# Later blocks of the routed experts loaded by plain transfers, and a planner that ranks small products behind indirect transfers

## The chip, the cores and the metric

The kernel runs on one core of one Trainium2 chip, as one program. The metric is the device time of one execution in microseconds. The time before is the median of 13 executions.

## The reference

A decoder of four layers works on 2048 tokens (32 sequences of 64) of width 256, in float32. Each layer adds three parts to the residual, each on its layer-normed input: a mixer, a cross attention, and a feed-forward part.

```python
x = x + L0_attn(ln(x)); x = x + L0_xattn(ln(x), ctx); x = x + L0_ffn(ln(x))   # attention, 32 heads
x = x + L1_attn(ln(x)); x = x + L1_xattn(ln(x), ctx); x = x + L1_ffn(ln(x))   # state space mixer; 8 experts, top 2
x = x + L2_attn(ln(x)); x = x + L2_xattn(ln(x), ctx); x = x + L2_ffn(ln(x))   # state space mixer
x = x + L3_attn(ln(x)); x = x + L3_xattn(ln(x), ctx); x = x + L3_ffn(ln(x))   # attention; 64 experts, top 6, room for 128
```

The part that the change touches is the feed-forward of layer 1. A router picks for each token the two best of eight experts and weighs them by a softmax over those two. Each expert is a gated unit of inner width 256 (gate clamped from above at 7, up part clamped to -7 to 7, the product `(up + 1) * gate * sigmoid(1.702 * gate)`), and the token receives the weighted sum of its two experts' outputs.

## The kernel before

**Tiles and groups.** The 2048 tokens are 16 tiles of 128 rows. They go through the layers in three groups of 8, 6 and 2 tiles (`GROUPS`). While one group goes through the later part of the network (the experts of layer 1, layers 2 and 3), the next one goes through layers 0 and 1: `weave` records the two streams alternately. The last group computes all eight experts for all its tokens (`unit_L1_expert`); the first two groups use queues, and only those two are touched by the change.

**The queues of layer 1.** `plan_L1_ffn` makes five kinds of steps for a group of nt tiles:

- `unit_L1_route`, one for two tiles: the router, the two best experts, each token's place in its expert's queue, and two indirect transfers for each tile by GpSimd that scatter the normed rows into the DRAM tensor `queue`. An expert's queue has `cap` = 128 nt rows and was filled with zeros beforehand.
- `unit_L1_blocks`, once: a block is 128 rows of one expert's queue. There are `blocks_of(tiles)` blocks, 23 for 8 tiles and 19 for 6. Block b below 8 is the first block of expert b. Which expert the blocks from 8 on belong to depends on the tokens; this step computes it on VectorE from the experts' counts: for each later block its expert `ex`, the first row `at` of its part of the queue, and from these two tables of indices, `st["weights"]` and `st["rows"]`, with one index for each of the 128 partitions.
- `unit_L1_block`, one for each block: loads the expert's weights `w` (128 partitions of 1540 floats: gate and up, down, biases) from `f1_rows` and 128 rows `xs` from the queue, transposes the rows, computes the expert and stores its output to the DRAM tensor `result`. Blocks 0 to 7 load by plain transfers issued on SyncE (SP). The later blocks, 15 in the first group and 11 in the second, load by two indirect transfers issued on GpSimd (POOL), `nc.gather`, with the indices of the tables.
- `unit_L1_result`, one for each tile: gathers the two results of each token by two indirect transfers and adds them, weighted, to the residual.

Layer 3's experts use indirect transfers as well: 84 scatters into `slots` (6 a tile in the first two groups) and 64 scatters into `parts`. In all there are 256 indirect transfers, all issued on GpSimd, of which 52 are the later blocks' loads.

**Buffers.** Every tile of SBUF and PSUM is one of a few kinds with a fixed number of slots (`SLOTS`): 9 of kind w (the blocks' weights among them), 16 of kind b2 (the blocks' rows), 8 banks of PSUM (mm).

**The planner.** The code only records operations. `in_turns` then orders them: `Order.run` is a list scheduler with a cost for each operation (`duration`), which at each step takes the operation with the smallest key over all five engines; the key is the time at which it could start, with additions for changes of tile shape on TensorE (`SWITCH`) or of activation tables on ScalarE. An operation may go to TensorE, VectorE, ScalarE, GpSimd or SyncE, some to either of two. Where the plan leaves TensorE idle for more than 1.6 us, `fill` puts in a spare product (`spare_mm`) whose output nobody reads. The planner runs five times forwards with backward passes in between and keeps the shortest plan; `issue` writes the instructions in that order, each engine's in its own queue, which is worked through in order. Semaphores do the rest: where the plan's times are wrong, only the order stays.

**Names in the profile.** All instructions are written by one line of `issue`, so every row says L2500, and rows are told apart by the buffers' names: `L_block_w` and `L_block_b` are the block's weights and its other buffers, `L_blocks_sm` and `L_blocks_b` the tables of `unit_L1_blocks`, `queue`, `result`, `slots` and `parts` the DRAM tensors. The layer's number is left out of names, so `L_attn_mm` are products of several layers' attention; those of form 32*64 are the scores of layer 0, 128 products for one tile, each on one of four 32-row strips of the array. A float32 product has two records of weight load and two of matmul, a transpose one of each.

Of the kernel before, what the change touches and what calls it, by code (L numbers as in the profile page):

```python
# [23 lines left out]
ALU = mybir.AluOpType  # L24
AX = mybir.AxisListType

P = 128
# [422 lines left out]
        return lambda *args, **kw: self.rec.add([(self.name, method)], args, kw)  # L450


DMA = ("dma_start", "indirect_dma_start")
TABLES = {"Exp": 1, "Ln": 2, "Sigmoid": 3, "Silu": 4, "Sin": 4}


def part(method, args):

    if method == "transpose":
        return 128, 128  # L460
    return tuple(32 if n <= 32 else 64 if n <= 64 else 128 for n in (args[1].n, args[1].size()))


def duration(engine, method, args, kw):

    out = kw["out"] if "out" in kw else args[0]
    if method in DMA:
        return 0.45 if engine == "sync" else 1.28
    views = [v for v in [*args, *kw.values()] if isinstance(v, View)]
    n = max(v.size() for v in views)  # L470
    if engine == "tensor":
        k, m = part(method, args)
        if method == "transpose":
            return 0.109
        n = args[2].size()
        if m == 128:
            return max(0.223, n * 0.00167 + 0.004) if k > 32 else max(0.056, n * 0.00053)
        if k == 128:
            return max(0.058, n * 0.00083 + 0.003) if m == 64 else max(0.055, n * 0.00043 + 0.008)
        return n * 0.00042 + 0.002 if k == 64 else n * 0.00021 + 0.001  # L480
    small = any(v.size() == 1 and v.n > 1 for v in views) and n > 1
    psum = any(v.t.psum for v in views)
    full = sum(all(s for s, _ in v.dims) and v.size() == n for v in views[1:])
    if engine == "vector":
        if not psum and method in ("tensor_scalar", "tensor_copy", "tensor_scalar_add", "tensor_single_scalar"):
            return 0.16 + n * 0.00052 + 0.11 * small
        if method.startswith("reduce") and views[1].dims[-1][0] > 1:
            return 0.15 + n * 0.0017
        return 0.15 + n * 0.00104 + 0.06 * small
    if engine == "scalar":  # L490
        if method == "activation":
            return (0.17 if psum else 0.205) + n * 0.00083 + 0.18 * (small and psum)
        return 0.16 + n * 0.00084 + 0.1 * small
    if method == "memset":
        return 0.2 + n * 0.00066
    if ALU.pow in args:
        return 0.4 + 0.157 * n
    if method == "tensor_copy":
        return 0.25 + n * 0.001
    return 0.14 + n * (0.00174 if full < 2 else 0.0022)  # L500
# [17 lines left out]
NEAR = 10  # L518


def combines(op, engine, method):

    if engine == "gpsimd":
        return method == "tensor_tensor" and ALU.pow not in op.args
    return engine == "vector" and not any(v.t.psum for v in op.outs + op.ins if isinstance(v, View))


class Order:
    ENGINES = ("tensor", "vector", "scalar", "gpsimd", "sync")

    def __init__(self, ops, slots, horizon, spare):
        self.ops, self.slots, self.horizon, self.spare = ops, slots, horizon, spare
        self.free_at = {e: 0.0 for e in self.ENGINES}
        self.table, self.moved = 0, 0.0
        self.part = None

        self.until = {"vector": 0.0, "gpsimd": 0.0}

        self.free = {tag: [(0.0, k) for k in range(n)] for tag, n in slots.items()}

        events = {tag: [] for tag in slots}
        for o in ops:
            for t in o.tiles:
                if t.tag in slots and t.first == o.at:
                    events[t.tag].append((o.at, 0, t))
                if t.tag in slots and t.last == o.at:
                    events[t.tag].append((o.at, 1, t))
        self.events = {tag: sorted(ev, key=lambda e: e[:2]) for tag, ev in events.items()}

        work, self.pos = 0.0, []  # L550
        for o in ops:
            self.pos.append(work)
            if o.ways[0][0] == "tensor":
                work += duration("tensor", o.ways[0][1], o.args, o.kw)
# [31 lines left out]
    def fill(self, o, start):  # L586
# [9 lines left out]
        t.slot = free.pop(at[-1])[1]  # L596
        return op

    def elsewhere(self, o, engine, since, end):


        for w, m in o.ways:
            if w != engine:
                other = max(self.free_at[w], since) + duration(w, m, o.args, o.kw)
                gain = {"vector": 1.0, "gpsimd": -1.0}[w] if {w, engine} == {"vector", "gpsimd"} else 0.0
                if other + gain < end:
                    return True
        return False

    def run(self):  # L610
# [10 lines left out]
        while not all(done[oldest:]):  # L621
            limit = self.pos[oldest] + self.horizon
            best = None
            for e in self.ENGINES:
                now, seen, first = self.free_at[e], 0, 1e9
                for o in ready[e]:
# [13 lines left out]
                    if e == "tensor":  # L640
                        if start == now:
                            first = min(first, self.pos[o.at])
                        if part(method, o.args) != self.part:
                            key += SWITCH
                            cost += SWITCH
                        elif self.pos[o.at] > first + NEAR:
                            key += SWITCH
                        elif self.part != (128, 128):
                            key = start
                    if e == "scalar":  # L650
                        table = TABLES.get(getattr(o.args[2], "name", "") if method == "activation" else "", 0)
                        if table and table != self.table:
                            key += 1.3
                            cost += 1.3
# [36 lines left out]
            if e == "scalar":  # L691
                m = next(m for w, m in o.ways if w == e)
                table = TABLES.get(getattr(o.args[2], "name", "") if m == "activation" else "", 0)
                self.table = table or self.table
            if e == "tensor":
                self.part = part(o.ways[0][1], o.args)
            lat = latency(e, o)
            if o.ways[0][1] in DMA:
                v = next(v for v in o.outs + o.ins if isinstance(v, View) and v.dtype != I32)
# [87 lines left out]
class Net:  # L787
# [985 lines left out]
    def unit_L1_blocks(self, st):  # L1773
# [15 lines left out]
        nc.vector.tensor_tensor(tmp, low, tb(nb, 8), ALU.mult)  # L1789
        nc.vector.reduce_sum(end, tmp, AX.X)  # L1790

        ex, before, last, at = self.sm(n), self.sm(n), self.sm(n), self.sm(n)
        over = self.tmp(n, 8)
        nc.vector.tensor_tensor(over, bc(io, 2, 8), tb(end, n), ALU.is_ge)
        nc.vector.reduce_sum(ex, over[:, :, :7], AX.X)
        st["weights"] = self.sm(n, dtype=I32)
        nc.vector.tensor_scalar(st["weights"], ex, float(P), self.k("row"), ALU.mult, ALU.add)
        nc.vector.tensor_tensor(over[:, :, :7], over[:, :, :7], tb(nb[:, :7], n), ALU.mult)
        nc.vector.reduce_sum(before, over[:, :, :7], AX.X)
        nc.vector.tensor_tensor(over, bc(ex, 2, 8), tb(e8, n), ALU.is_equal)  # L1800
        nc.vector.tensor_tensor(over, over, tb(count, n), ALU.mult)
        nc.vector.reduce_sum(last, over, AX.X)

        nc.vector.scalar_tensor_tensor(at, io, 1.0, before, ALU.add, ALU.subtract)
        nc.vector.tensor_scalar(at, at, float(P), self.k("row"), ALU.mult, ALU.add)
        nc.vector.scalar_tensor_tensor(at, last, -1.0, at, ALU.add, ALU.min)
        nc.vector.tensor_single_scalar(at, at, 0.0, ALU.max)
        st["rows"] = self.sm(n, dtype=I32)
        nc.vector.scalar_tensor_tensor(st["rows"], ex, float(st["cap"]), at, ALU.mult, ALU.add)
# [15 lines left out]
    def unit_L1_block(self, b, st):  # L1825
        nc = self.nc
        w, xs = self.w(1540), self.b2(256)
        if b < 8:
            self.load(w, self.ins["f1_rows"][b * P : (b + 1) * P, :])
            self.load(xs, st["queue"](b * st["cap"], b * st["cap"] + P))  # L1830
        else:
            nc.gather(w, self.ins["f1_rows"], st["weights"][:, b - 8 : b - 7])
            nc.gather(xs, st["queue"](), st["rows"][:, b - 8 : b - 7])
        gu, dn, bias = w[:, :1024].rearrange("p (c n) -> p c n", c=2), split(w[:, 1024:1536], 2), w[:, 1536:]
        xT = self.b2(2, P)
        ps = split(self.mm()[:, :256], 2)
# [643 lines left out]
def issue(tc, order, slots):  # L2480
# [3 lines left out]
    with ExitStack() as ctx:  # L2484
# [9 lines left out]
        for op, e in order:  # L2494
            for t in op.tiles:
                if t.real is None:
                    tag = t.tag if t.slot is None else f"{t.tag}_{t.slot}"
                    t.real = pools[t.pool].tile(t.shape, t.dtype, name=t.name, tag=tag)
            method = next(m for w, m in op.ways if w == e)
            done = getattr(getattr(nc, e), method)(*map(real, op.args), **{k: real(v) for k, v in op.kw.items()})  # L2500
            if op.group is not None:
                op.name = done.ins.name
                tc.add_to_no_dep_group(op.group, done.ins)
                tc.declare_no_dep(done.ins, group=op.group, reason="rows of their own")

            for o in op.behind:
                if o.group != op.group and (e, o.name) not in waited:
                    waited.add((e, o.name))
                    tc.add_manual_dep(done.ins, o.name, sync, reason="rows")
# [99 lines left out]
```

## Time and profile before

| | |
|---|---|
| median of 13 executions | 2955.72 us (2953.68 to 2965.59) |
| profiled execution | 2956.93 us |
| its span, first to last instruction | 2955.2 us |
| mean granted TensorE clock | 0.979 |
| busy PE / PEld | 2885.5 us (98%) / 2401.2 us (81%) |
| busy DVE / ACT / POOL | 2046.7 us (69%) / 1415.4 us (48%) / 1485.1 us (50%) |
| DMA | 257.26 MB, mean 87 GB/s |
| queue q1, plain transfers (hardware_dynamic) | 204.73 MB, 19.9% of 16 engines |
| queue q0, indirect transfers (software_dynamic) | 48.01 MB, 4.7% |
| queue q8, instructions | 230 packets, 3.77 MB, 0.5% |
| spare products | 138 records, 34.3 us of PE |

PE is TensorE's matmul, PEld its weight load, DVE VectorE, ACT ScalarE, POOL GpSimd, SP SyncE. A group's line has the engine, the operation, the buffers written and read, the number of instructions, and their times. In a timeline, the bracket at the end of a line is the engine's idle time before the instruction and what ended it; "issue" stands for idle time in which the engine waited for nothing that the profile shows. The granted clock is the share of TensorE's full clock; in this trace it is either 1 or 0.5 at a time, and a mean over a stretch lies between.

### The profile page before, as it was taken

The numbers are of one execution on the slowest core, as the hardware profiler recorded it, in microseconds if no ns is written. First come the engines' busy times: TensorE is split into PE (matmuls) and PEld (weight loads), VectorE is DVE, ScalarE is ACT, GpSimd is POOL, SyncE is SP. The second block draws the span as 40 slices with busy tenths as digits, with TensorE's granted clock in tenths as the row PEclk, the third lists the DMA queues.
The fourth block names the chain that finished last, engine by engine and source line by source line (L and its number), as shares of the span: only waits on it lengthen the run. The fifth ranks groups of instructions, "written<-read, shape, count | busy, mean of one in ns | idle before, by whom it ended". The sixth has DMA issues, their size and how long they took to land.

```text
span 2955.2 us, 70820 instructions
## 1 busy us (share of the span) xinstructions
PE 2885.5 (98%) x29064; PEld 2401.2 (81%) x29064; DVE 2046.7 (69%) x5046; ACT 1415.4 (48%) x2665; POOL 1485.1 (50%) x1334
## 2 busy tenths in 40 slices
PE   9999999999999999999999999999999999998899
PEld 8888888787878888878888788878897878887677
DVE  5554337775666557765588998887756778898863
ACT  2224225565543233454466666665335565466460
POOL 5542143222765545523667536676554557555561
PEclk8999999999999999999999999999999999999899
DMA  5002421301251244412001010022374122221255
GB/s 187 13 10 94 169 72 43 144 1 45 104 210 44 62 139 137 138 38 81 32 30 38 25 42 30 6 89 85 114 261 142 56 95 81 63 76 39 78 162 204
DMA packets 112966, 257.26 MB, mean 87 GB/s; under 512 B 26309, under 2 KB 73688, under 8 KB 100228
## 3 DMA queue, kind: packets, MB, share of 16 engines
q1 hardware_dynamic: 97860, 204.73, 19.9%
q0 software_dynamic: 14784, 48.01, 4.7%
q8 instruction: 230, 3.77, 0.5%
q14 instruction: 92, 0.75, 0.1%
HBM read 177.34 MB, written 78.77 MB: 87 GB/s over the span
## 4 chain that ended last, share of the span: by engine, by line
PE 86%; DVE 8%; issue 2%; ACT 2%; POOL 1%; DMA 1%; POOLq 0%; DVEq 0%; ACTq 0%
PE L_xattn_mm L2500 13%; PE ssm_heads_mm L2500 10%; PE cross_out_mm L2500 9%; PE L_attn_mm L2500 9%; PE pair_mm L2500 9%; PE L_ffn_mm L2500 5%; PE rope_mm L2500 5%; PE turn_mm L2500 4%; PE L_block_mm L2500 3%; PE cross_scores_mm L2500 2%; PE L_dense_mm L2500 2%; DVE ssm_heads_b L2500 2%; PE heads_mm L2500 1%; PE L_experts_mm L2500 1%; PE small_scores_mm L2500 1%
## 5 line engine op out<-in xcount | busy, mean ns | idle before, releaser
L2500 PE MATMUL pair_mm<-norm_b,load_ssm_w 128*128 128x256 f32 x1280 | 306.3, 381 | 1.5 <-DVE L_attn_b L2500 0.8
L2500 PEld LDWEIGHTS pair_mm<-norm_b,load_ssm_w 128*128 128x128 f32 x1280 | 236.0, 190 | 41.8 <-issue 10.5
L2500 ACT COPY turn_b<-turn_mm 128x512 f32<-128x512 f32 x264 | 145.2, 592 | 149.8 <-PE turn_mm L2500 148.1
L2500 DVE SCALAR_TENSOR_TENSOR ssm_heads_b<-pair_mm,load_ssm_wp,ssm_heads_b 128x252 f32<-128x252 f32 (+2 forms) x480 | 196.1, 463 | 21.5 <-ACT ssm_heads_b L2500 19.8
L2500 POOL TENSOR_TENSOR L_xattn_sm<-L_xattn_sm,__init___consts 128x8 f32<-128x8 f32 (+2 forms) x64 | 190.1, 2975 | 29.5 <-DVE L_xattn_sm L2500 26.8
L2500 ACT ACT_TABLE_LOAD x147 | 188.6, 1283 | 24.3 <-PE ssm_heads_mm L2500 7.0
L2500 ACT COPY L_xattn_b<-L_xattn_mm 128x512 f32<-128x512 f32 x172 | 101.2, 591 | 164.6 <-PE L_xattn_mm L2500 153.6
L2500 POOL TENSOR_TENSOR norm_sm<-norm_sm,__init___consts 128x1 f32<-128x1 f32 (+1 forms) x149 | 94.1, 637 | 153.9 <-DVE norm_sm L2500 124.5
L2500 PE MATMUL ssm_heads_mm<-load_ssm_w,ssm_heads_b 128*128 128x256 f32 x640 | 164.7, 387 | 1.2 <-POOL L_xattn_b L2500 1.2
L2500 PE MATMUL rope_mm<-norm_b,load_L_attn_w 128*128 128x128 f32 x1280 | 163.8, 281 | 0.7 <-ACT L_block_b L2500 0.5
L2500 PEld LDWEIGHTS rope_mm<-norm_b,load_L_attn_w 128*128 128x128 f32 x1280 | 155.9, 196 | 7.6 <-issue 4.6
L2500 POOL TENSOR_TENSOR ssm_heads_b<-ssm_heads_b,ssm_heads_b 128x1024 f32<-128x1024 f32 x31 | 75.4, 2437 | 146.2 <-DVE ssm_heads_b L2500 102.1
L2500 PEld LDWEIGHTS ssm_heads_mm<-load_ssm_w,ssm_heads_b 128*128 128x128 f32 x640 | 115.0, 190 | 31.8 <-issue 17.8
L2500 POOL TENSOR_TENSOR L_attn_b<-rope_b 128x256 f32<-128x256 f32 x147 | 105.4, 741 | 60.0 <-DVE rope_b L2500 51.0
L2500 ACT COPY norm_b<-norm_mm 128x256 f32<-128x256 f32 (+1 forms) x128 | 54.3, 437 | 168.0 <-PE norm_mm L2500 120.6
L2500 POOL TENSOR_TENSOR heads_b<-heads_b,heads_sm 128x1024 f32<-128x1024 f32 x49 | 96.3, 1973 | 75.9 <-DVE heads_sm L2500 54.5
L2500 PEld LDWEIGHTS L_xattn_mm<-norm_b,load_L_xattn_w 128*128 128x128 f32 x1024 | 121.9, 192 | 7.7 <-issue 5.0
L2500 PE MATMUL L_xattn_mm<-norm_b,load_L_xattn_w 128*128 128x128 f32 x1024 | 127.2, 276 | 0.8 <-ACT heads_b L2500 0.8
L2500 PE MATMUL L_xattn_mm<-norm_b,units_L_xattn_w 128*128 128x128 f32 x1024 | 124.8, 279 | 0.0
L2500 PEld LDWEIGHTS L_xattn_mm<-norm_b,units_L_xattn_w 128*128 128x128 f32 x1024 | 121.9, 195 | 3.0 <-issue 1.5
L2500 PE MATMUL cross_out_mm<-load_L_xattn_w,cross_out_b 128*128 128x256 f32 x512 | 122.3, 384 | 0.1
L2500 ACT ACTIVATE ssm_heads_b<-ssm_heads_b 128x512 f32<-128x512 f32 (+1 forms) x120 | 91.8, 773 | 62.6 <-DVE ssm_heads_b L2500 41.9
(432 smaller groups left out, 7783.7 us busy)
## 6 DMA issues: line engine op xcount, KB each, us to landing
queue<-far_w SPq DMA_DIRECT2D x14, 1024.0 KB, 12.6
L_block_w<-in_f_rows SPq DMA_DIRECT2D x16, 770.0 KB, 4.6
load_ssm_w<-in_s_in SPq DMA_DIRECT2D x12, 1024.0 KB, 7.2
parts<-far_w SPq DMA_DIRECT2D x10, 1024.0 KB, 13.8
slots<-far_w SPq DMA_DIRECT2D x16, 548.0 KB, 6.7
L_experts_b<-slots SPq DMA_DIRECT2D x32, 274.0 KB, 3.7
units_L_xattn_w<-kept_x SPq DMA_DIRECT2D x8, 1024.0 KB, 7.8
L_parts_b<-parts SPq DMA_DIRECT2D x14, 512.0 KB, 6.1
```

Source lines behind the costliest of these rows:

```text
L2500: done = getattr(getattr(nc, e), method)(*map(real, op.args), **{k: real(v) for k, v in op.kw.items()})
```

## The change

It has two parts. In the first, the later blocks' weights and rows are loaded by `dma_from`, a plain transfer on SyncE whose first row is read at run time: SyncE reads one index from the table into a register, and the transfer's source begins at that row. The tables now hold each block's first row (the per-partition addition goes), the clamp to the last token of the expert is replaced by a clamp to the last 128 rows of the expert's part of the queue, and the four instructions that computed and applied `last` go. A transfer may thus read queue rows that no token was written to; they hold zeros, and no token takes its result from them. The planner counts 0.9 us on SyncE for such a transfer.

In the second, the planner keeps a list `rows` of the planned indirect transfers and a model of TensorE's instruction supply: 80 instructions in stock, refilled at 11.3 a microsecond during such a transfer. A product is called small if its instructions (4, or 2 for a transpose) are more than that rate delivers in its planned duration. While the latest planned indirect transfer runs, a small product's key rises by `AVOID` = 3.0 us plus the modelled wait; an indirect transfer's key rises by `HOLD` = 1.5 us if TensorE's latest product was small.

```diff
-DMA = ("dma_start", "indirect_dma_start")
+DMA = ("dma_start", "indirect_dma_start", "dma_from")
...
-        return 0.45 if engine == "sync" else 1.28
+        return 0.9 if method == "dma_from" else 0.45 if engine == "sync" else 1.28
...
+AHEAD, SLOW = 80, 11.3
+AVOID, HOLD = 3.0, 1.5
+def instructions(method):
+    return 2 if method == "transpose" else 4
...
+    def supply(self, start):
+        ahead, at = self.ahead, self.at
+        for a, b in self.rows:
+            if b > at and a < start:
+                if a > at:
+                    ahead, at = AHEAD, a
+                b = min(b, start)
+                ahead, at = min(AHEAD, ahead + (b - at) * SLOW), b
+        if at < start:
+            ahead = AHEAD
+        return ahead
...
+                        if self.rows and self.rows[-1][1] > start:
+                            n = instructions(method)
+                            wait = max(0.0, n - self.supply(start)) / SLOW
+                            if n > duration(e, method, o.args, o.kw) * SLOW:
+                                key += wait + AVOID
+                            start += wait
+                    if e == "gpsimd" and method in DMA and self.light:
+                        key += HOLD
...
+            if e == "gpsimd" and m in DMA:
+                self.rows = [r for r in self.rows if r[1] > self.free_at["tensor"] - 5.0] + [(start, got)]
             if e == "tensor":
-                self.part = part(o.ways[0][1], o.args)
+                self.part, n = part(o.ways[0][1], o.args), instructions(m)
+                self.light = n > duration(e, m, o.args, o.kw) * SLOW
+                self.ahead, self.at = max(0.0, self.supply(start) - n), start
...
-        nc.vector.tensor_scalar(st["weights"], ex, float(P), self.k("row"), ALU.mult, ALU.add)
+        nc.vector.tensor_single_scalar(st["weights"], ex, float(P), ALU.mult)
...
-        nc.vector.tensor_tensor(over, bc(ex, 2, 8), tb(e8, n), ALU.is_equal)
-        nc.vector.tensor_tensor(over, over, tb(count, n), ALU.mult)
-        nc.vector.reduce_sum(last, over, AX.X)
...
-        nc.vector.tensor_scalar(at, at, float(P), self.k("row"), ALU.mult, ALU.add)
-        nc.vector.scalar_tensor_tensor(at, last, -1.0, at, ALU.add, ALU.min)
+        nc.vector.tensor_scalar(at, at, float(P), float(st["cap"] - P), ALU.mult, ALU.min)
...
-            nc.gather(w, self.ins["f1_rows"], st["weights"][:, b - 8 : b - 7])
-            nc.gather(xs, st["queue"](), st["rows"][:, b - 8 : b - 7])
+            at = slice(b - 8, b - 7)
+            nc.sync.dma_from(out=w, in_=self.ins["f1_rows"], row=st["weights"][:1, at], last=7 * P)
+            nc.sync.dma_from(out=xs, in_=st["queue"](), row=st["rows"][:1, at], last=8 * st["cap"] - P)
...
+            if method == "dma_from":
+                at = nc.sync.value_load(kw.pop("row"), min_val=0, max_val=kw.pop("last"))
+                kw["in_"], method = kw["in_"][bass.ds(at, P), :], "dma_start"
```

More of the change, by code (lines that the diff above doesn't have):

```diff
@@ L534, in __init__ @@
         self.table, self.moved = 0, 0.0
-        self.part = None
+        self.part, self.light = None, False
         self.until = {"vector": 0.0, "gpsimd": 0.0}
+        self.rows, self.ahead, self.at = [], AHEAD, 0.0
         self.free = {tag: [(0.0, k) for k in range(n)] for tag, n in slots.items()}
@@ L1790, in unit_L1_blocks @@
         nc.vector.reduce_sum(end, tmp, AX.X)
-        ex, before, last, at = self.sm(n), self.sm(n), self.sm(n), self.sm(n)
+        ex, before, at = self.sm(n), self.sm(n), self.sm(n)
         over = self.tmp(n, 8)
@@ L2499, in issue @@
             method = next(m for w, m in op.ways if w == e)
-            done = getattr(getattr(nc, e), method)(*map(real, op.args), **{k: real(v) for k, v in op.kw.items()})
+            kw = {k: real(v) for k, v in op.kw.items()}
+            if method == "dma_from":
+                at = nc.sync.value_load(kw.pop("row"), min_val=0, max_val=kw.pop("last"))
+                kw["in_"], method = kw["in_"][bass.ds(at, P), :], "dma_start"
+            done = getattr(getattr(nc, e), method)(*map(real, op.args), **kw)
             if op.group is not None:
```

## The prediction

> **What bounds the kernel now.** I read the page first, then the table of stages, then the views of the gathers, PE's waits and the timeline. All times are of one execution: 2956.93 us, span 2955.2 us, so 1.7 us lie around the span. The median of the runs before is 2955.72 us, 1.2 us lower; I carry differences from the trace over to that median. A difference below 0.2% (5.9 us) counts as no change, about what measurement can tell here.
>
> The page (busy time, granted clock in 40 slices, chain that ended last):
>
> ```profile
> PE 2885.5 (98%) x29064; PEld 2401.2 (81%) x29064; DVE 2046.7 (69%) x5046; ACT 1415.4 (48%) x2665; POOL 1485.1 (50%) x1334
> ...
> PEclk8999999999999999999999999999999999999899
> ...
> PE 86%; DVE 8%; issue 2%; ACT 2%; POOL 1%; DMA 1%; POOLq 0%; DVEq 0%; ACTq 0%
> ```
>
> TensorE is the bound; GpSimd, SyncE and transfers hardly lie on the chain. So work taken off GpSimd is worth nothing by itself: gains come from PE's idle 70 us (2955.2 - 2885.5) and from lost clock. The table of stages (us; busy per engine; granted clock; DMA share, GB/s) shows where:
>
> ```profile
> 930.00:1250.00 320.00, 309.67 (x3540) 274.66 (x3539) 214.11 (x524) 105.45 (x200) 166.43 (x167) 0.93 0.33 109
> ...
> 1925.00:2270.00 345.00, 339.08 (x3274) 284.39 (x3273) 233.03 (x645) 159.49 (x319) 211.63 (x194) 0.98 0.43 148
> ...
> 2680.00:2955.20 275.20, 248.93 (x2366) 196.54 (x2348) 183.69 (x599) 118.82 (x243) 130.93 (x134) 0.93 0.37 125
> ```
>
> These are the three stages with indirect transfers. Lost clock there: 0.07 x 320 = 22 us, 0.02 x 345 = 7 us, 0.07 x 275 = 19 us. The last has also 26 us of idle PE. This is the ground the change can win or lose on.
>
> **Part 1: 52 gathers become plain transfers.** The tile view of the gathers and the list of DMA issues (last number: us to landing):
>
> ```profile
> L2500 POOL DMA_INDIRECT L_block_w<-in_f_rows,L_blocks_sm x26: 940/961/1947, 1084.0 to 2190.5; - x26
> ...
> L2500 POOL DMA_INDIRECT L_block_b<-queue,L_blocks_sm x26: 945/971/1162, 1015.2 to 2193.9; - x26
> ...
> L_block_w<-in_f_rows SPq DMA_DIRECT2D x16, 770.0 KB, 4.6
> ...
> L_block_w<-in_f_rows,L_blocks_sm POOLq DMA_INDIRECT x26, 7.3
> ```
>
> Removed from GpSimd: 26 x 0.96 + 26 x 0.97 = 50 us, in two stretches (about 1015 to 1182 and 2153 to 2195). GpSimd's waits put 19.0 us before weight gathers for a buffer that PE frees; products queued behind them on GpSimd (halves of rope, row scalings) come free earlier. On the path this is 0: POOL is 1% of the chain. What counts is where PE stood still. PE's waits in 1000:1200, and two lines of the timeline:
>
> ```profile
> PE L_attn_mm L2500 <- issue: 2.2, 1, 2.2
> PE L_block_mm L2500 <- DVE L_block_b L2500: 2.0, 1, 2.0
> PE L_block_mm L2500 <- DMA L_block_w<-in_f_rows,L_blocks_sm: 1.3, 1, 1.3
> ```
>
> ```profile
> 1113.43 3.16 DVE L2500 SCALAR_TENSOR_TENSOR L_block_b<-L_block_b,L_block_b 128x256 f32<-128x256 f32 x2
> ...
> 1116.40 1.97 PE L2500 MATMUL L_block_mm<-L_block_w,L_block_b 128*128 128x256 f32 x8 [2.04 <-DVE L_block_b L2500]
> ```
>
> (a) 1.3 us waiting for gathered weights. A plain load lands 7.3 - 4.6 = 2.7 us sooner, so the wait goes: 1.3 us, between 0 and 1.3. (b) A VectorE product took 2.8 us instead of its median 0.42 beside the gather at 1113.05, and PE waited 2.0 us for it: 2.0 us, between 0 and 2.0, since GpSimd's own products can stretch it as well. (c) The 2.2 us of "issue" at 1101.4 to 1103.6 are a late fetch of PE's instructions. The DMA queues from 1092.7 to 1101.1, and behind it from 1101.1 to 1105.5:
>
> ```profile
> q0 software_dynamic: 329, 1.68, 57.6%
> q1 hardware_dynamic: 720, 0.87, 29.4%
> ```
>
> ```profile
> q8 instruction: 2, 0.03, 3.0%
> ```
>
> While gathers hold q0, no instruction fetch starts for 8.4 us; then two come, and PE has run dry. A 10.2 us stretch (1101.0 to 1111.2) at clock 0.50 follows, 5.1 us lost. But small products run dry without gathers too: the same strip group at 161.3 waited 1.60 us for instructions and lost no clock. So of 2.2 + 5.1 = 7.3 us I give the gathers 2.2 - 1.6 + 5.1 = 5.7, between 0 and 7.3. In the second stretch PE waits for no transfer: 0. Sum: 1.3 + 2.0 + 5.7 = 9.0 us, between 0 and 10.6.
>
> Added: 52 register reads and 52 transfers on SyncE. The trace of before shows no register read. Bounds: one issue on SyncE (0.33 us, the plain weight load) and the landing of a small transfer (2.7 us, the block's rows from the queue); I take 1.5, 52 x 1.5 = 78 us of SyncE over some 210 us, where it mostly waits (ACT's L_block_b alone holds it 77 us in 1000:1200). Behind the new waits on SyncE stand result stores, context loads and the next mixer's weights; PE waits for those late by no line of this stretch. So 0 on the path; if that cover fails, a late load costs about the 1.3 us of (a), and four of them 5 us. (The Trainium skill, "DMA: Bandwidth & Descriptors", section "Latency and other measured facts", puts a register load's floor near 600 ns; by that SyncE would get an estimated 31 us instead. No run here shows it.) The eight small VectorE instructions dropped in the two block plans, 0.16 to 0.28 us each, are off the path: 0.
>
> **Part 2: the planner's ranking.** While a planned indirect transfer runs, products that it calls small (128 columns, strips, transposes) get 3 us on their key and a modelled stall; a GpSimd transfer gets 1.5 us after such a product. No instruction is added; the written order changes. The model says 11.3 instructions per us, with 80 in stock. The timeline beside the last experts' scatters speaks against that rate:
>
> ```profile
> 2859.24 3.67 PEld L2500 LDWEIGHTS L_experts_mm<-L_experts_b,load_L_experts_w 128*32 128x32 f32 x136 [0.33 <-ACT L_experts_b L2500]
> ```
>
> ```profile
> 2858.82 0.97 POOL L2500 DMA_INDIRECT parts<-L_experts_b,L_experts_sm  x1 [0.30 <-DMA parts<-L_experts_b,L_experts_sm]
> 2860.10 0.97 POOL L2500 DMA_INDIRECT parts<-L_experts_b,L_experts_sm  x1 [0.30 <-DMA parts<-L_experts_b,L_experts_sm]
> ```
>
> 136 weight loads with their matmuls are 272 instructions in 3.67 us, 74 per us. So the cost avoided is rare, tied to large gathers, and Part 1 takes those away. (The Trainium skill, "Runtime: NRT & Kernel Launch", section "Instruction fetch mechanics", says a sequential program's fetch is hidden; by it the ranking would win 0. The trace agrees beside these scatters but not at 161.3 and 1101.) The one place left where it may help: strips beside the result gathers at 1205 wait 1.2 us and are followed by 6.9 us at clock 0.51, together 1.2 + 3.4 = 4.6 us. I take half, 2 us, between 0 and 4.6.
>
> The larger unknown is the reordering itself: every order is planned anew. Two rows of the windows table show what an order is worth (busy PE, then weight loads, GpSimd and clock):
>
> ```profile
> 1007.00:1012.30 5.30, 5.30 (x212) 5.29 (x213) 2.49 (x7) 0.00 (x0) 0.73 (x1) 1.00 0.11 28
> 161.30:165.90 4.60, 3.14 (x255) 3.00 (x256) 2.01 (x3) 0.00 (x0) 1.42 (x2) 1.00 0.02 5
> ```
>
> The same score products of the first attention: 213 weight loads in 5.3 us, against 256 in 3.0 us of loading. At 161 the four 32-row strips alternate, at 1007 one strip follows another, presumably as score banks come free. Slow ones are followed by 13.6 us at clock 0.50. A new plan can mend or make several such groups: I price it from -20 to +20 us, with 0 as the value taken.
>
> Sum: 9.0 + 2 + 0 = 11 us less: 2956.9 - 11 = 2946 in the profiled execution, 2955.7 - 11 = 2945 against the median.
>
> **The rivals.** R1, luckier orders: the strips of 1007 and 1095 alternate again. At full clock 213 weight loads took 5.3 us there and 221 took 6.2 (1095.2 to 1101.4); at 3.0 us per 256 they take 2.5 and 2.6, so 2.8 + 3.6 = 6.4 us go, and of the 13.6 us at clock 0.50 another 6.8: 2945 - 13 = 2932. For it: both stand where the plan changes most. Against: nothing in the ranking counts strips. R2, covered: a plain load moves the same 770 KB on the same engines, delays the same fetch, and VectorE stalls go elsewhere: 2955. R3, slower, one mechanism: the 3 us let PE wait, or run spare products, for a large product that is almost ready while a small one is ready. Its place is the tail from 2680, where 100 indirect transfers remain, PE lacks work (26 us idle, 15.6 us of spares) and the small products feed ACT and DVE. If one transfer in eight costs 1.5 us, 19 us, and three further half-clock stretches of 6.9 us cost 10, that is 29, less 9 of Part 1: 2955.7 + 20 = 2976. It decides from seven such holds on (7 x 1.5 = 10.5, about the gain). Against it: where no large product is near, the small one still starts first.
>
> **How the numbers follow.** Forecast 0.42 (own range 2936 to 2954), R1 0.13, R2 0.14, R3 0.31. Beyond 5.9 us faster means below 2949.8: of the forecast 0.36, all of R1, 0.01 of R2: 0.50. Within: 0.06 of the forecast, 0.10 of R2, 0.01 of R3: 0.17. The rest is slower: 0.33. The range reaches past R1 and R3 by part of the reordering's spread: 2918 to 2979.
>
> **What would show it.** Right: 204 indirect transfers instead of 256; block weights only from SyncE, landing near 5 us; no PE wait for gathered weights; clock above 0.93 in the first routed stage; the tail not longer than 275 us. Wrong: a tail of 285 us or more with more spares and a clock under 0.93 (R3); PE waiting for block loads from SyncE (register reads dear); or "issue" waits of 2 us beside the plain loads (R2).

## The result, and the profile after

The changed kernel takes 2990.76 us (median of 9, 2984.39 to 3001.66), the kernel before 2956.66 us (median of 40, 2949.65 to 2965.59): a ratio of 1.0116, 95% interval 1.0105 to 1.0127, or 34 us slower. The prediction was 11 us faster, 2945, with 2979 as its upper end.

The page of the changed kernel (span 2987.8 us, granted clock 0.974), busy time first, then the clock in 40 slices, then the two data queues:

```profile
PE 2901.1 (97%) x29064; PEld 2408.2 (81%) x29064; DVE 2040.7 (68%) x5019; ACT 1422.3 (48%) x2667; POOL 1461.3 (49%) x1306
...
PEclk8999999999999999999999999999999999999899
...
q1 hardware_dynamic: 105348, 228.64, 22.1%
q0 software_dynamic: 9792, 24.10, 2.3%
```

Half of the indirect bytes have moved to q1, as the change says. The work of TensorE is the same 29064 products, 138 of them spares as before. Its span is 32.6 us longer, and two sums account for that. Idle time: 2987.8 - 2901.1 = 86.7 against 69.7 us, 17.0 more. Lost clock: 0.026 x 2987.8 = 77.7 against 0.021 x 2955.2 = 62.1 us, 15.6 more. The stages (as in the prediction: length, busy per engine, clock, DMA share, GB/s):

```profile
930.00:1250.00 320.00, 312.58 (x3591) 276.39 (x3590) 228.27 (x588) 119.93 (x224) 152.09 (x155) 0.95 0.35 111
1925.00:2270.00 345.00, 331.56 (x3282) 278.98 (x3282) 223.25 (x615) 148.71 (x295) 185.18 (x183) 0.98 0.40 138
2680.00:2987.80 307.80, 273.60 (x2581) 218.11 (x2580) 197.94 (x611) 139.78 (x287) 158.74 (x155) 0.92 0.35 117
```

In the first routed stage TensorE does more than before (3591 matmuls against 3540, clock 0.95 against 0.93). The third window starts at 2680 us in both kernels and runs to the end, so that its 307.8 - 275.2 = 32.6 us are the whole loss by definition and don't say where it arose. The last product of the last block does, before and then after:

```profile
L2500 PE MATMUL L_block_mm<-L_block_w,L_block_b x168: 379/379/631, 1051.9 to 2233.0; 128*128 128x256 f32 x168
L2536 PE MATMUL L_block_mm<-L_block_w,L_block_b x168: 379/379/634, 1032.5 to 2233.2; 128*128 128x256 f32 x168
```

It starts at 2233.0 us and at 2233.2, and by 2270 us TensorE has done nearly the same number of products (22677 and 22658 by the windows): behind all the changed loads the two kernels stand level. The stretch from 2270 to 2680 us, before and then after, and one group of products and the next indirect transfers, in the same order:

```profile
2270.00:2680.00 410.00, 402.59 (x4049) 330.42 (x4049) 340.38 (x841) 243.34 (x479) 237.31 (x214) 1.00 0.21 70
2270.00:2680.00 410.00, 401.70 (x3835) 328.47 (x3834) 331.29 (x811) 239.98 (x460) 219.42 (x193) 0.97 0.20 67
```

```profile
L2500 PE MATMUL ssm_heads_mm<-load_ssm_w,ssm_heads_b x128: 379/379/483, 2295.3 to 2648.8; 128*128 128x256 f32 x128
L2500 POOL DMA_INDIRECT slots<-norm_b,L_ffn_sm x36: 967/974/1908, 2729.9 to 2788.5; - x36
```

```profile
L2536 PE MATMUL ssm_heads_mm<-load_ssm_w,ssm_heads_b x128: 379/379/483, 2294.2 to 2669.6; 128*128 128x256 f32 x128
L2536 POOL DMA_INDIRECT slots<-norm_b,L_ffn_sm x36: 967/978/1317, 2714.3 to 2817.1; - x36
```

In the same 410 us TensorE does 214 products fewer, about 21 us at the mean of 0.1 us for one (an estimate, since products differ), and 0.03 x 410 = 12 us go to the clock; the group of 128 products starts 1.1 us earlier and ends 20.8 us later. No indirect transfer starts between 2260 and 2714 us in either trace. So some 20 of the 32.6 us are lost where nothing that the change is about takes place: no load that changed, and no indirect transfer beside which the ranking acts. Only the order differs there.

The new loads themselves, from the tile view of the weights and the view of the line that reads the register (ns minimum/median/maximum, first and last start):

```profile
L2536 SPq DMA_DIRECT2D L_block_w<-in_f_rows x42: 327/338/377, 911.9 to 2194.1; - x42
```

```profile
L2534 SPq TENSOR_LOAD <-L_blocks_sm x52: 262/268/872, 1044.3 to 2204.8; - x52
L2534 SPq FUSED_REGOPS  x52: 152/152/177, 1044.8 to 2205.1; - x52
L2534 SPq SEQ_ASSERT  x52: 18/18/33, 1045.0 to 2205.3; - x52
```

The three instructions of a read last 0.268 + 0.152 + 0.018 = 0.44 us, but gaps come with them. Five such loads issued one behind the other:

```profile
1045.36 4.97 SPq L2536 DMA_DIRECT2D L_block_b<-queue  x5
```

They stand (4.97 - 0.34) / 4 = 1.16 us apart, 0.34 us of it the issue itself, so a read holds SyncE some 0.8 us. The weights land 4.6 us after their issue, in the median. TensorE waits 0.3 us in all for block weights from a transfer, 1.3 before; its waits for VectorE and ScalarE have grown, by the sums of all rows from 16.4 to 28.6 us and from 27.1 to 36.6 us. Some of the rows:

```profile
PE L_attn_mm L2536 <- issue: 15.4, 10, 2.0
PE small_scores_mm L2536 <- ACT keys_apart_b L2536: 7.6, 5, 2.9
...
PE L_block_mm L2536 <- DVE L_block_b L2536: 3.9, 3, 1.5
...
PE norm_mm L2536 <- DVE norm_b L2536: 2.9, 5, 1.0
...
PE L_route_mm L2536 <- DVE L_route_sc L2536: 2.4, 1, 2.4
```

The last two rows name waits that the profile before lists nowhere at this size. The "issue" waits, which the ranking takes for late instructions and is meant to avoid, are as before, 15.4 against 15.3 us for `L_attn_mm`: it removed none of their sum.

One place shows what a new order does. At the end of layer 1's second group GpSimd gathers the results of twelve transfers one behind the other, and TensorE has spare products until the next norm. Timelines of TensorE, before and then after:

```profile
2252.92 7.07 PE L2500 MATMUL spare_mm<-__init___consts 128*128 128x256 f32 x32
2259.83 0.60 PE L2500 MATMUL norm_mm<-__init___consts,norm_b 128*128 128x128 f32 x4
```

```profile
2250.82 13.11 PE L2536 MATMUL spare_mm<-__init___consts 128*128 128x256 f32 x60
2263.76 0.60 PE L2536 MATMUL norm_mm<-__init___consts,norm_b 128*128 128x128 f32 x4
```

6.0 us more of empty products stand here, though GpSimd starts its gathers 1 us earlier (2241.8 against 2242.8), and the norm comes 3.9 us later. (In the whole kernel the spare products take 34.7 us against 34.3: the place shows what an order moves about, and is no account of the 32.6 us.) VectorE's residual additions that take the gathered results start 5.9 us later, at 2252.2 instead of 2246.3:

```profile
L2500 DVE SCALAR_TENSOR_TENSOR __init___x<-L_result_b,plan_L_ffn_rt,__init___x x12: 449/475/485, 2246.3 to 2263.8; 128x256 f32<-128x256 f32 x12
```

```profile
L2536 DVE SCALAR_TENSOR_TENSOR __init___x<-L_result_b,plan_L_ffn_rt,__init___x x12: 453/476/479, 2252.2 to 2262.0; 128x256 f32<-128x256 f32 x12
```

All ratios below compare with the kernel before, measured beside each run. Beside the result, e17 and e18 it took 2957 us (condition A), beside e1 to e16 3062 to 3073 us (condition B); the last section shows how the two differ.

### The profile page after: what moved, and what is told of

Its sections match the earlier page's. It is cut to its first block, busy times and chain, and to the rows that moved or that the text cites. A ratio compares the mean times of both kernels' runs of the same rounds, so it can differ in the third digit from the quotient of the medians.

```text
span 2987.8 us, 71043 instructions
## 1 busy us (share of the span) xinstructions
PE 2901.1 (97%) x29064; PEld 2408.2 (81%) x29064; DVE 2040.7 (68%) x5019; ACT 1422.3 (48%) x2667; POOL 1461.3 (49%) x1306
## 5 line engine op out<-in xcount | busy, mean ns | idle before, releaser
L2536 ACT COPY turn_b<-turn_mm 128x512 f32<-128x512 f32 x249 | 137.1, 593 | 142.1 <-PE turn_mm L2536 133.8
L2536 PEld LDWEIGHTS rope_mm<-norm_b,load_L_attn_w 128*128 128x128 f32 x1280 | 152.9, 193 | 10.6 <-issue 7.7
L2536 POOL TENSOR_TENSOR L_attn_b<-rope_b 128x256 f32<-128x256 f32 x156 | 111.7, 741 | 57.3 <-DVE rope_b L2536 54.4
L2536 DVE TENSOR_TENSOR rope_b<-rope_mm,__init___consts 128x512 f32<-128x512 f32 x160 | 103.3, 680 | 30.0 <-PE rope_mm L2536 22.2
```

## The experiments

The theories, as the expectations name them: TRANSFERS, the new loads cost; ORDER, the new written order does. Of the order: RANKING, the planner's new rules are bad for this kernel; LOTTERY, any new plan moves the time, whatever its rules.

**The order or the transfers (e1, e2).** The two kernels differ in how blocks are loaded and in the written order. e1 keeps every engine's order of before and only swaps the loads (with the new clamp of the row); e2 keeps the changed order and swaps them back.

```diff
 e1: in issue(), order of before
+if "last" in kw:
+    at = nc.sync.value_load(index[:1], min_val=0, max_val=kw["last"])
+    e, method, kw = "sync", "dma_start", {"out": kw["out"], "in_": kw["in_"][bass.ds(at, P), :]}
 e2: in issue(), order of after
+if method == "dma_from":
+    e, method = "gpsimd", "indirect_dma_start"    # 128 indices, one for each partition
```

> The order of every engine as before, instruction for instruction; only the 52 later-block loads are issued by SyncE as plain transfers with a register's row, at the same place of the order, and the clamp of the queue's row is the new one. Theory ORDER (the loss lies in the newly written order, the plain transfers gain what the prediction's terms a to c say): 2940 to 2952 us, 3 to 12 us under before. Theory TRANSFERS (register reads on SyncE and late loads cost): 2970 us or more. Theory LOTTERY (any new order moves the time by tens of us, whatever is changed): as ORDER here, since the order stays.

> The order of every engine as in the changed kernel; only the 52 later-block loads are issued by GpSimd as gathers again, at the same place of the order, with one index for each partition. Theory ORDER: 2990 us or more, as the changed kernel or a few us above it. Theory TRANSFERS: near 2957, the loss gone.

Measured: e1 0.995 (0.993 to 0.997), 3057.37 us; e2 1.0156 (1.0131 to 1.0181), 3123.98 us. Plain transfers gain and the written order loses, whichever loads go with it. TRANSFERS falls.

**Each part alone, planned anew (e3, e4).**

```diff
 e3: the change without the ranking
-if self.rows and self.rows[-1][1] > start:
+if False and self.rows and self.rows[-1][1] > start:
-AVOID, HOLD = 3.0, 1.5
+AVOID, HOLD = 3.0, 0.0
 e4: the planner of the change, with unit_L1_blocks and unit_L1_block of before
```

> Part 1 alone: plain transfers, planned anew without the ranking of small products, without the hold and without the modelled stall. Theory ORDER, in the form that the ranking makes the bad order: 2940 to 2955 us. Theory TRANSFERS: 2980 us or more. Theory LOTTERY: anywhere within 20 us of before on either side, with the gains and losses spread over stages that hold no indirect transfer too.

> Part 2 alone: gathers as before, planned with the ranking, the hold and the modelled stall. Theory ORDER with the ranking as its cause: 2975 to 3000 us, most of the loss. Theory TRANSFERS: within 6 us of before. Theory LOTTERY: anywhere within 20 us of before.

Measured: e3 0.9932 (0.9908 to 0.9957); e4 0.9986 (0.997 to 1.0001). The parts don't add up: neither alone loses, both together do.

**The changed kernel again, and orders drawn anew (e5, e6, e7).** A "draw" alters one planned duration by 0.01 us or less; the rules stay, and the work but for the number of spare products, and the plan comes out different.

```diff
 e5: the changed kernel;  e6: e5 and, e7: before, with
-return ... 0.45 if engine == "sync" else 1.28
+return ... 0.46 if engine == "sync" else 1.28
```

> The changed kernel itself, beside the others of this call, so that its ratio and theirs come from one chip. Both theories expect 1.010 to 1.013 against before if this chip is like the one of the result; if it is one on which before takes 3.07 ms, with e2 at 1.0156 there and plain transfers worth 0.5% (e1), the sum gives 1.010 to 1.011.

> The changed kernel with one number of the planner altered that has nothing to do with the change: an issue on SyncE is planned at 0.46 us instead of 0.45. The rules of the ranking stay. RANKING (the rules that put small products later beside GpSimd's transfers make the order worse, by about 1.7% with the plain transfers' gain taken out) expects 1.007 to 1.015 against before. LOTTERY (any new order moves the time by up to 1.5% to either side, and the changed kernel drew a bad one) expects a time that differs from the changed kernel's by more than 0.4%, most likely 0.99 to 1.005 against before.

> The kernel before with the same one number altered (SyncE's issue planned at 0.46 us), neither part of the change in it. RANKING expects 0.998 to 1.002, since without the ranking the orders are alike. LOTTERY expects a difference of 0.3% to 1% to either side.

Measured: e5 1.009 (1.0073 to 1.0107), e6 1.0076 (1.0055 to 1.0097), e7 1.0019 (1.0006 to 1.0032). So far this spoke for RANKING: LOTTERY had expected both redraws to move by more. With e1, e2 and e5 the square of loads and orders is closed: the changed order costs 1.0156 with gathers and 1.009 / 0.995 = 1.014 with plain loads, 42 to 46 us of 2957.

**Which part of the ranking (e8, e10, e11).**

```diff
 e8:  AVOID, HOLD = 0.0, 1.5
 e11: AVOID, HOLD = 6.0, 1.5
 e10:
     key += wait + AVOID            # a small product beside an indirect transfer
+elif start > now:                  # a large one that is not ready yet
+    key += AVOID
```

> The changed kernel with the 3 us on a small product's key set to 0; the modelled stall and the 1.5 us on a GpSimd transfer stay. RANKING, in the form that the 3 us are the harm, expects the level of plain transfers without ranking (e3: 0.993), 0.990 to 0.996. If the modelled stall is the harm, the time stays at 1.007 to 1.013. LOTTERY expects no relation to either.

> The changed kernel, in which beside a planned indirect transfer a large product that is not yet ready gets the same 3 us as a small one, so that TensorE is never planned to wait for a large product while a small one is ready; small ones still go behind large ones that are ready. HOLD-UP (the prediction's R3: TensorE waits for a large product that is almost ready) expects the loss to go: 0.993 to 1.000 against before. FEED (the small products put late feed VectorE, ScalarE and the chains of the next steps, and it does not matter what runs in their place) expects 1.005 to 1.013.

> The changed kernel with 6 us instead of 3 on the key of a small product beside an indirect transfer. With 0 us it was at 0.9949 (e8), with 3 us at 1.009 (e5). If the push itself is the harm, more of it costs more: 1.012 to 1.025. If 3 us already puts every small product behind all that could go first, it stays at 1.006 to 1.012. LOTTERY expects anything from 0.99 to 1.015.

Measured: e8 0.9949 (0.9928 to 0.9971); e10 0.9971 (0.9954 to 0.9988); e11 1.0131 (1.0104 to 1.0158). Read alone, this is a clean story: the 3 us do the harm, more with 6, none with 0, and R3's mechanism (TensorE held up for a large product) is the reason. The draws below do not bear it out.

**The ranking with gathers again, and before's trace (e9, e12).**

```diff
 e9: e4 with 0.46 for 0.45;  e12: the kernel before
```

> The ranking alone with GpSimd's gathers, as in e4, and SyncE's issue planned at 0.46 us instead of 0.45, which draws another order. e4 was at 0.9986 against before, while both parts together are at 1.009 (e5) and 1.0076 with another draw (e6). RANKING (the ranking costs about 1.4% whatever loads the blocks) expects 1.004 to 1.014 and says that e4 was a lucky draw. PAIR (the ranking harms only where the plain loads leave GpSimd free) expects 0.995 to 1.002 again.

> The kernel before itself, for its trace on the chip of these runs: the ratio is 1.000 within 0.3%. If plain transfers gain by the three terms of the prediction (the wait for gathered weights, a VectorE product stretched beside a gather, a late fetch of instructions), this trace shows more idle time of TensorE between 1000 and 1260 us than e1's, in the same order, by some 5 to 15 us, and hardly a difference elsewhere.

Measured: e9 0.9944 (0.9926 to 0.9962); e12 1.0009 (0.9996 to 1.0021). e12 and e1 have the same order, so their traces price Part 1, with two reservations: they come from two chips of condition B, and e1's profiled execution is the fastest of its six, 5 us under their median. TensorE's waits from 930 to 1340 us, e12 and then e1:

```profile
PE L_attn_mm L2500 <- issue: 7.0, 12, 1.5
PE L_block_mm L2500 <- DVE L_block_b L2500: 1.5, 1, 1.5
PE L_block_mm L2500 <- DMA L_block_w<-in_f_rows,L_blocks_sm: 1.3, 1, 1.3
```

```profile
PE L_attn_mm L2510 <- issue: 4.1, 9, 1.2
PE L_block_mm L2510 <- DVE L_block_b L2510: 1.4, 1, 1.4
```

And the same stretch of nearly the same products by the windows, e12 and e1:

```profile
975.00:1332.00 357.00, 344.48 (x3504) 299.07 (x3503) 231.65 (x563) 132.64 (x239) 160.60 (x163) 0.94 0.32 106
```

```profile
973.00:1320.00 347.00, 338.56 (x3498) 294.03 (x3497) 226.66 (x562) 132.31 (x239) 131.25 (x133) 0.95 0.33 108
```

Ten us shorter: the wait for gathered weights (1.3) is gone, "issue" costs 2.9 less, and lost clock falls from 0.06 x 357 = 21.4 to 0.05 x 347 = 17.4 us, some 4 (the two-place clock leaves it 2 or 3 us either way). That is about 8 of the 10. More than half of it lies in the one strip group that the prediction's term (c) names, here in e12 and then in e1, up to the norm behind it:

```profile
1098.37 1.78 PE L2500 MATMUL L_attn_mm<-L_attn_b,L_attn_b 32*64 32x64 f32 x53
...
1103.27 9.09 PE L2500 MATMUL L_attn_mm<-L_attn_b,L_attn_b 32*64 32x64 f32 x189 [1.10 <-issue]
1112.29 0.47 PE L2500 MATMUL norm_mm<-__init___consts,norm_b 128*128 128x128 f32 x1
```

```profile
1095.91 8.43 PE L2510 MATMUL L_attn_mm<-L_attn_b,L_attn_b 32*64 32x64 f32 x256
1104.27 0.47 PE L2510 MATMUL norm_mm<-__init___consts,norm_b 128*128 128x128 f32 x1
```

The same 256 products take 13.9 us with four "issue" waits in e12, and 8.4 us without any in e1: 5.6 us. The wait for VectorE stays, 1.5 and 1.4 us. The two VectorE products ahead of it take 3.16 us in e12 beside a gather and a product of GpSimd's own, and 2.45 in e1 beside that product alone:

```profile
1111.52 2.45 DVE L2510 SCALAR_TENSOR_TENSOR L_block_b<-L_block_b,L_block_b 128x256 f32<-128x256 f32 x2
1111.28 2.08 POOL L2510 TENSOR_TENSOR L_attn_b<-L_attn_b,shift_sm 128x1024 f32<-128x1024 f32 x1
```

The expectation for e12 is met in part: TensorE's idle time in the stretch is 12.5 against 8.4 us, 4.1 and not 5 or more, and the traces differ elsewhere too, 20.6 us over the whole span. The tail, where no block is loaded, is shorter too (from 2689 us on 378 us in e12, from 2675 us on 372 in e1, clock 0.83 and 0.86); nothing in the change accounts for that, and one execution of each can't tell it from the spread of e1's six (3052 to 3065 us).

**Second and third draws (e13 to e16).**

```diff
 e13: the changed kernel, e16: e4, with
-return 0.109          # a transpose
+return 0.110
 e14: e10, e15: e8, with 0.46 for 0.45
```

> The changed kernel, third draw: a transpose planned at 0.110 us instead of 0.109, the ranking as it is. RANKING (the 3 us are bad for this kernel with plain loads) expects 1.004 to 1.014, like e5 (1.009), e6 (1.0076). LOTTERY expects a draw from 0.993 to 1.014, with as much chance below 1.002 as above.

> e10 (0.9971) in a second draw, SyncE's issue planned at 0.46 us. HOLD-UP (the harm is TensorE planned to wait for large products not yet ready) expects 0.993 to 1.001 again. LOTTERY, or FEED with e10 as a lucky draw, expects 1.002 to 1.013.

> e8 (plain loads, no push of small products; 0.9949) in a second draw, SyncE's issue planned at 0.46 us. RANKING and HOLD-UP expect 0.992 to 0.998. LOTTERY expects 0.993 to 1.010. If it stands below 0.995 it is the version to take instead of the change.

> The ranking with GpSimd's gathers, third draw, a transpose planned at 0.110 us. e4 and e9 gave 0.9986 and 0.9944. PAIR (the ranking harms only with plain loads) expects 0.993 to 1.000. LOTTERY, by which e4 and e9 were two good draws, expects up to 1.012.

Measured: e13 0.9857 (0.9825 to 0.9889), e14 0.993 (0.9908 to 0.9953), e15 0.988 (0.9851 to 0.9908), e16 1.0167 (1.0137 to 1.0197). e13 is the change with all its rules and by its ratio the fastest kernel here; e16, gathers with the same rules, the slowest. RANKING and PAIR fall as causes of the loss: the same rules gave 1.009, 1.0076 and 0.9857 with plain loads, and 0.9986, 0.9944 and 1.0167 with gathers. HOLD-UP met its numbers twice, yet the rule that it mends gave a faster kernel still in e13, so that it is the cause is not shown. LOTTERY's own ranges were missed as well, in e13, e15 and e16 by moves larger than it allowed (e15 also lies below the range of RANKING and HOLD-UP): what the runs show is that a draw outweighs the rules, and not how wide the draws are. SyncE's planned issue altered by 0.01 us moved the time by 0.1 to 0.7% (e6, e7, e9, e14, e15), the planned transpose by 2.3% and 1.8%, once down and once up (e13 against e5, e16 against e4).

Where a lucky and an unlucky draw differ is seen in the pages of e5 (span 3090.8, clock 0.957) and e13 (3043.1, 0.963):

```profile
PE 2951.6 (95%) x29064; PEld 2432.8 (79%) x29064; DVE 2041.6 (66%) x5019; ACT 1424.6 (46%) x2667; POOL 1459.4 (47%) x1306
```

```profile
PE 2923.8 (96%) x29022; PEld 2417.4 (79%) x29022; DVE 2053.5 (67%) x5038; ACT 1421.5 (47%) x2670; POOL 1435.7 (47%) x1284
```

Idle time is 139.2 against 119.3 us (19.9 more), lost clock 0.043 x 3090.8 = 132.9 against 0.037 x 3043.1 = 112.6 (20.3 more): 40 of the 47.7 us, in the same two halves as after against before. Most of the rest is in 42 spare products fewer (96 against 138, 25.2 against 38.8 us of PE, in part the same time as the lost clock). By medians e13's gain is larger still: its profiled execution is the slowest of its four (3023 to 3045 us). At the place shown above, e13's plan has other products to run while the results are gathered; its spares before the norm are 12:

```profile
2265.30 14.08 PE L2536 MATMUL cross_out_mm<-units_L_xattn_w,cross_out_b 128*128 128x256 f32 x64
2279.22 2.75 PE L2536 MATMUL spare_mm<-__init___consts 128*128 128x256 f32 x12
2282.05 0.76 PE L2536 MATMUL norm_mm<-__init___consts,norm_b 128*128 128x128 f32 x4
```

**A last draw of each (e17, e18).**

```diff
 e17: the changed kernel, 0.44 for 0.45;  e18: e3, a transpose at 0.110
```

> The changed kernel, fourth draw: SyncE's issue planned at 0.44 us, the ranking as it is. The draws so far are 1.009, 1.0076 and 0.9857. LOTTERY (each draw falls somewhere in 0.985 to 1.017) expects a draw anywhere there, most likely between 0.995 and 1.010. If the push of small products costs on the average, the mean of the four stays above 1.000: this one above 0.998.

> Plain loads without any ranking, a transpose planned at 0.110 us: another draw of e3 (0.9932), beside e1 (0.995, the old order) and the draws without the push, e8 (0.9949) and e15 (0.988). If the spread of draws is narrower without the push than with it, this one lies between 0.986 and 0.998. If the spread is the planner's alone, it can lie up to 1.010.

Measured, beside a kernel before of 2956.94 us: e17 1.0159 (1.012 to 1.0198), 3006.2 us; e18 1.0106 (1.0063 to 1.0149), 2988.22 us. e18 has no ranking at all and loses as much as the changed kernel: the push of small products is not needed for a loss of 1%, as by e13 it isn't enough for one.

## Why the prediction was wrong

**The step that failed** is the term for the reordering: "from -20 to +20 us, with 0 as the value taken". By e1, e2 and e5 the changed order costs 42 to 46 us, whichever loads go with it. Thirteen newly planned orders in condition B lay from 0.9857 (e13) to 1.0167 (e16), 44 us below before to 51 us above. The term was mis-sized by a factor of more than two, and it alone decided the sign. It was priced from two strip groups of layer 0's attention; the change plans all 29064 products anew, and idle time and lost clock move in other stages as well: some 20 of the 32.6 us between the traces arise from 2270 to 2680 us, outside the three stages with indirect transfers that the prediction calls "the ground the change can win or lose on". The same rules with one planned duration altered wrote an order 44 us faster than before (e13), so that this one is slow is in good part the luck of the draw; whether the ranking adds to it on the average is open.

**Part 1** was right in sign and nearly in size. Predicted 9.0 us (0 to 10.6); e1 against before, in condition B, gives 0.5%, 15.8 us between the medians, with an interval of 9 to 22, and the traces show 10 us in the stage named, one execution each. By its terms: (a) the wait for gathered weights, 1.3 predicted, 1.3 gone; (b) the VectorE product stretched beside a gather, 2.0 predicted, 0.1 gone: without the gather the product is still stretched, beside a product of GpSimd's own, as the lower end of the term allowed; (c) late instructions and the half clock behind them, 5.7 predicted, 5.6 gone at the place named and 2.9 + 4.0 = 6.9 in the whole stretch.

**The register reads** lay off the path, as said, but their price was off: 1.5 us taken, some 0.8 measured, 52 of them 42 us and not 78. (The Trainium skill, "DMA: Bandwidth & Descriptors", section "Latency and other measured facts", puts the load's floor near 600 ns; here the load's own row has a median of 268 ns, and the measurement decides.)

**Part 2's own gain**, 2 us from supply waits avoided, isn't seen: 15.4 us of "issue" after, 15.3 before. In condition B, where such waits are many, the ranking did not lessen them either: the sums of "issue" in TensorE's waits are 43.9 to 69.7 us in the seven traces whose order was planned with all its rules (e2, e4, e5, e6, e9, e13, e16), and 48.0 to 60.0 in the four without (e1, e3, e7, e12).

**The rivals.** R3 (slower, 2976) came nearest in time; its mechanism is not shown. Two of its signs hold, a tail over 285 us (307.8) and a clock below 0.93 there (0.92), but the first holds for any loss of 10 us or more, since the tail is counted from a fixed 2680 us. The third, more spares, hardly does (138 in both kernels; 66 against 64 in the tail). R3 saw its place in the tail, beside 100 indirect transfers; some 20 of the 32.6 us were lost ahead of it, beside none. R1's lucky order is not what was drawn, though it exists: e13 beats before by more than R1 allowed. Of the signs for "right", 204 indirect transfers, weights from SyncE landing near 5 us, hardly a wait for them (0.3 us) and a clock above 0.93 in the first routed stage were met, and said nothing of the sign: they test Part 1.

**Open.** Whether the push also shifts the mean of the draws: with plain loads its four draws are 1.009, 1.0076, 0.9857 and 1.0159, those without it 0.9932, 0.9949 (e8), 0.988 (e15) and 1.0106, too few and from two conditions. And why all three new orders timed where before takes 2957 us lost 1.1 to 1.6%, while eight of the thirteen timed in condition B were below 1. What drops the clock between 2270 and 2680 us in the changed order is open. The fastest versions, e13 and e15, and e1, which keeps the old order, ran only in condition B; whether they beat the kernel before in condition A wasn't tried.

## What to carry to other kernels

Where a planner writes the whole order, an edit of its rules is a redraw of the order: price that draw first, by several neutral redraws, and give it the width they show, ahead of any effect of a few us. One redraw is too few: the only one of the kernel before (e7) moved it by 0.2%, while the newly planned orders here spread some 1.5% to either side. Test such a rule on several draws; one pair of runs, even with intervals of 0.2%, compares two orders and not two rules. To judge the part that does not need a new order, issue it into the old one, as e1 does.

## What the runs showed of the hardware

The same program, the kernel before, has two conditions 4% apart: 2956.94 us beside e17 (A), 3074.86 us as e12 (B). Between the traces of before and e12 the span grows by 115.8 us: lost clock makes 0.044 x 3071.0 - 62.1 = 73 us of it, "issue" waits 53.7 - 15.3 = 38. The end of the experts in e12, by TensorE's waits from 2680 us on and by the window of the same bounds as before's last:

```profile
PE L_experts_mm L2500 <- issue: 16.1, 26, 2.0
```

```profile
2680.00:2955.00 275.00, 230.85 (x2300) 172.35 (x2302) 181.14 (x582) 132.92 (x266) 134.47 (x132) 0.81 0.23 71
```

There TensorE has 26 "issue" waits in products that stand among GpSimd's scatters; in the trace of before from the prediction that row doesn't occur, and the clock in that window is 0.93. (By 2680 us e12 is behind and does other work in the window; over all of its rest, 391 us, its clock is 0.83.) If "issue" stands for late instructions here, as the prediction read it, the shortage that the planner models does show beside these scatters, in one condition and not in the other, for the same instructions in the same order. (The Trainium skill, "Runtime: NRT & Kernel Launch", section "Instruction fetch mechanics", has the fetch hidden for a sequential program; so read, e12 speaks against it, and the faster condition beside the scatters does not.) What sets the condition is not known from these runs; the chip's number alone does not, since chip 6 is on record with both (before at 3062 us beside e5 to e8, at 2957 us beside e17 and e18).
